# Layer 0 of a two-layer perceiver: where Newton's square root runs, five decode steps for fourteen, and the order of a turn

## The chip, the core and the metric

The kernel runs on one core of one Trainium2 chip, written in Bass with the Tile framework. The metric is the device time of one launch in microseconds (us), median of several runs. The engines are named as in the profile: PE (TensorE, matmuls), DVE (VectorE), ACT (ScalarE), POOL (GpSimd) and SP (SyncE, here only a queue that issues DMAs).

## What is computed

The input x is 64 sequences of 32 places with 256 features, and each sequence has a context of 257 places. Six blocks are added to x one after the other, each on its layer norm. Cut to what matters here:

```
def _layernorm(x, axis=-1, eps=1e-05):
    return (x - m) / jnp.sqrt(v + eps)
...
x = x + _L0_xattn_ref(_layernorm(x, axis=-1), ctx_1024, ctx_1024, ...)
x = x + _L0_attn_ref(_layernorm(x, axis=-1), ...)
x = x + _L0_ffn_ref(_layernorm(x, axis=-1), ...)
x = x + _L1_xattn_ref(_layernorm(x, axis=-1), ctx_1024, ctx_1024, ...)
x = x + _L1_attn_ref(_layernorm(x, axis=-1), ...)
x = x + _L1_ffn_ref(_layernorm(x, axis=-1), ...)
return x
```

The first is a cross-attention with 16 heads of 16 and a causal window, so that only the first 32 places of the context count; the second a causal self-attention of the same shape; the third a linear layer with inputs and weights in fp8 (e4m3). Layer 1 has a cross-attention over all 257 places, a gated mixer and a mixture of one shared and the best 2 of 8 experts. The fp8 weight comes as bytes and is decoded on the chip: sign, four exponent bits and three mantissa bits become a number. In both attentions of layer 0 keys and queries are turned by the rotary tables: `near * cos + far * sin`, where `far` is the partner feature.

## The kernel before

The 2048 rows of x are four tiles `xs[g]` of 512 rows. `small_attentions` (L246) runs both attentions of layer 0 as one pipeline over eight groups: `order` lists (attention 0, g = 0 to 3) and then (attention 1, g = 0 to 3). A group n has four turns, t = 0 to 3; each turn scores 128 rows. All instructions of layer 0 are kept in the order in which the program issues them, on each engine (`InOrder`, `kept`), and `line` carries the last tiles from turn to turn. In a turn the loop (L560 to L626) does this for different tiles at once:

- `turned` (transposes of e, ps_t, copied to eT by ACT) and, at the turn's end, `context` (ps_o, then o on DVE) for the tile of two turns ago; `by_feature` (transposes of o, ps_c, copied to cT by ACT) for the one of three turns ago; `project` (ps_p, added to x by DVE) for the one of four turns ago.
- `rotated` for the group after: keys in t 0 and 1, queries in t 2 and 3. PE makes ps_qk, DVE `part` (times sin), SP copies `part` to `far` with four DMAs, ACT makes `near`, POOL multiplies it by cos. The addition `near + far` into kT or qT, on POOL, is returned as a function and issued one turn later (`adds`, `due`), behind the next turn's own `near` except at t = 0. Before the first group everything of `rotated` but far and the sum is on DVE.
- `spread_keys`: kT times the heads' masks into kb, three of four on ACT, one on POOL.
- `values` for the group after, at t 0 and 2: ps_v, copied to v by ACT, written to `v_rows` by SP; `blocks` reads them back into the block-diagonal vb, four DMAs for each half, both halves at t = 3.
- `norm_steps` for the group after the next: mean and variance on DVE (st, mv), then 1/sqrt by three Newton steps on 128x4 numbers (ve, half, r, sq, rn), then y on DVE. Newton runs on DVE for the first two groups and in group 0, otherwise on POOL. `prepare` takes a step at t 0, 1, 2 and 3 each. `opened` transposes y (psT) into yT at t = 3.
- `scores` (pair_bank; mx and sc on DVE; e on ACT), and `sums` for the last tile (sm on DVE).
- `decode_fp8`: a step at t 0 and 2, in groups 6 and later at every t. It has fourteen steps, seven for each of two halves of 256 columns, in the tile `scratch`; the result is w8.

In group 6 the fp8 layer's own steps for rows 0 (`first_sides`) come in, and from group 7 on `cross_attention` takes over PE, two steps a turn: keys and values of the last context place, the four pieces of the first keys (`keys`), queries. After the pipeline, cross-attention, mixer and experts follow from 237 us on. `first_loads` is a generator of DMAs on SP: three steps before the loop, then one a turn at t 1 to 3.

Of the kernel before, what the change touches and what calls it, by code (L numbers as in the profile page):

```python
# [16 lines left out]
P = 128  # L17
# [47 lines left out]
def perceiver_kernel(ctx: ExitStack, tc: tile.TileContext, a: dict, out: bass.AP):  # L65
# [54 lines left out]
    def turn(ps, src, eye):  # L120
        return kept(nc.tensor.transpose(ps, src, eye))  # L121

    def norm_steps(g, eng=None, apart=False, ts=range(NT), by_act=False):

        x = xs[g]
        n, t0 = len(ts), ts[0]
        st = small.tile([P, n, 6], F32, tag="st", name="st")
        mv = small.tile([P, n, 2], F32, tag="mv", name="mv")
        for t in range(n):
            vector.bn_stats(st[:, t, :], x[:, t0 + t, :])  # L130
        if apart:
            yield
        for t in range(n):
            vector.bn_aggr(mv[:, t, :], st[:, t, :])

        ve = small.tile([P, n], F32, tag="ve", name="ve")
        vector.tensor_scalar(ve, mv[:, :, 1], EPS, None, ALU.add)
        half = small.tile([P, n], I32, tag="half", name="half")
        vector.tensor_scalar(half, ve.bitcast(I32), 1, None, ALU.logical_shift_right)
        r0 = small.tile([P, n], I32, tag="r0", name="r0")  # L140
        vector.tensor_scalar(r0, half, -1.0, float(0x5F3759DF), ALU.mult, ALU.add)
        r = r0.bitcast(F32)
        for _ in range(3):
            sq = small.tile([P, n], F32, tag="sq", name="sq", bufs=6)
            rn = small.tile([P, n], F32, tag="rn", name="rn", bufs=6)
            if eng is vector:
                vector.tensor_tensor(sq, r, r, ALU.mult)
                vector.scalar_tensor_tensor(sq, sq, -0.5, ve, ALU.mult, ALU.mult)
                vector.scalar_tensor_tensor(rn, sq, 1.5, r, ALU.add, ALU.mult)
            else:  # L150
                gpsimd.tensor_tensor(sq, r, r, ALU.mult)
                gpsimd.tensor_tensor(sq, sq, ve, ALU.mult)
                gpsimd.tensor_scalar(sq, sq, -0.5, 1.5, ALU.mult, ALU.add)
                gpsimd.tensor_tensor(rn, sq, r, ALU.mult)
            r = rn
        if by_act:
            off = small.tile([P, n], F32, tag="off", name="off")
            gpsimd.tensor_scalar(off, mv[:, :, 0], -1.0, 1.0, ALU.mult, ALU.mult)
            gpsimd.tensor_tensor(off, off, r, ALU.mult)
        yield  # L160
        y = ypool.tile([P, n, D], F32, tag="y", name="y")
        for t in range(n):
            if by_act:
                scalar.activation(
                    y[:, t, :],
                    x[:, t0 + t, :],
                    AF.Identity,
                    bias=off[:, t : t + 1],
                    scale=r[:, t : t + 1],
                )  # L170
            else:
                vector.tensor_scalar(
                    y[:, t, :],
                    x[:, t0 + t, :],
                    mv[:, t, 0:1],
                    r[:, t : t + 1],
                    ALU.subtract,
                    ALU.mult,
                )
            if t == 1 and n > 2:  # L180
                yield
        return y
# [63 lines left out]
    def small_attentions(layers, first_loads, decode, sides, load_layer1, layer1):  # L246
# [54 lines left out]
            if not it["from_ctx"]:  # L301
                it["kvT"] = yT

        def rotated(it, i, c):

            src, cs, sn = (
                (it["kvT"], cos, sin) if i == 1 else (it["yT"], cosq, sinq)
# [5 lines left out]
            w, v0 = it["w"], it["v0"]  # L313
            ps = pa([P, GT], "ps_qk")
            proj(ps, lambda k: w[:, i, k, c * P : (c + 1) * P], lambda k: src[:, k, :])

            def by_place(table):
                return table.rearrange("p (o q) -> p o q", o=1).to_broadcast([P, 16, S])
# [2 lines left out]
                return tile_.rearrange("p (b q) -> p b q", q=S)  # L321

            bias = vec[:, v0 + 2 * i + c : v0 + 2 * i + c + 1]
            part = part_([P, GT], "part")
            vector.scalar_tensor_tensor(
                by_seq(part), by_seq(ps), bias, by_place(sn), ALU.add, ALU.mult
            )
# [2 lines left out]
            for at in range(0, P, S):  # L330
                queue = scalar if (it["n"], i, c) == (0, 0, 1) and at >= 2 * S else sync
                queue.dma_start(out=far[at : at + S, :], in_=part[at ^ S : (at ^ S) + S, :])
            near = near_([P, GT], "near")
            if it["n"] > 0:
                scalar.activation(near, ps, AF.Identity, bias=bias)
                gpsimd.tensor_tensor(by_seq(near), by_seq(near), by_place(cs), ALU.mult)
# [166 lines left out]
        it = group(0, fetch(0))  # L503
        next(loads)
        after = group(1, fetch(1))
        next(loads)
        for half in range(2):
            clear(vbs[0][half], vector)
            clear(vbs[1][half], gpsimd)
# [5 lines left out]
        opened(it)  # L515
        mask(1)
        vector.tensor_tensor(eye, ident[:, 0:S], ident[:, 64 : 64 + S], ALU.add)
        steps = norm_steps(order[1][1], vector, apart=True)
        next(steps)
        adds.append(rotated(it, 1, 1))  # L520
        adds[0]()
# [1 line left out]
            spread_keys(it, 0, 0, part)  # L523
        adds.append(rotated(it, 0, 0))
        adds.append(rotated(it, 0, 1))
        adds[1]()
        for part in range(2):
            spread_keys(it, 0, 1, part)
# [1 line left out]
            add()  # L530
        for pair in range(2):
            values(it, pair)
        after["y"] = finish(steps)
        for half in range(2):
            blocks(it, half)
        now = it


# [3 lines left out]
        for n in range(len(order) + 1):  # L542
# [3 lines left out]
                after["kb"] = [None, None]  # L546
            kvT = coming = None
            if n + 2 <= last:
                side = norm_steps(order[n + 2][1], None if n else vector, apart=True)
            else:  # L550
                side = sides

            def prepare(at):
                if n + 2 <= last and at:
                    try:
                        next(side)
                    except StopIteration as end:
                        return end.value

            for t in range(NT):  # L560
                if line[2]:
# [2 lines left out]
                if n <= last:  # L564
                    if t < 2:
                        kb_now = (now, 1, t)
                    elif after is not None:
                        kb_now = (after, 0, t - 2)
                due, adds = adds, []
                if t == 0:  # L570
                    for add in due:
                        add()
                    due = []
                if kb_now:
                    spread_keys(*kb_now, 0)
                if line[4]:
# [1 line left out]
                if after is None:  # L578
                    next(layer1, None)
                else:  # L580
                    y = prepare(t % 2 == 1)
                    adds.append(rotated(after, *((1, 0), (1, 1), (0, 0), (0, 1))[t]))
                if line[3]:
                    by_feature(line[3])
                prepare(t % 2 == 0)
                if n + 2 > last:
                    next(side, None)
                    next(side, None)
                if n > 0:
                    add_bias(n - 1, t)  # L590
                if n > 0 and (t % 2 == 0 or n + 2 > last):
                    next(decode, None)
                for add in due:
                    add()
                if kb_now:
                    spread_keys(*kb_now, 1)
                if after is None:
                    next(layer1, None)
                elif t % 2 == 0:
                    values(after, t // 2)  # L600
                    if (n, t) == (0, 0):
                        opened(after)
                elif t == 3:
                    for half in range(2):
                        blocks(after, half)
                    if n + 2 <= last:
                        coming = group(n + 2, kvT)
                        coming["y"] = y
                        opened(coming)
                line[0] = scores(now, t) if n <= last else None  # L610
                if (n, t) == (last, NT - 1):
                    pair_pool.close()
# [19 lines left out]
    def first_loads():  # L632
# [12 lines left out]
        sync.dma_start(out=xs[1], in_=x_view[1])  # L645
        yield
        sync.dma_start(out=xs[2], in_=x_view[2])
        sync.dma_start(out=w_cur[:, 3], in_=a["w_l0x"][:, 3])
        row_load(R_XO0)
        sync.dma_start(out=xs[3], in_=x_view[3])  # L650
        yield
        sync.dma_start(out=raw, in_=a["w_fp8"])
        for at in (R_AO0, R_FF, R_XO1, R_GO):
            yield
            row_load(at)
        for i in range(0, 4, 2):
# [9 lines left out]

    def decode_fp8():

        scratch = sb.tile([P, 4, D], F32, tag="yT", name="scratch")
        u, neg, e_f, scale = (scratch[:, i, :] for i in range(4))  # L670
        bits = scale.bitcast(I32)
        for c in range(2):
            vector.tensor_copy(u, raw[:, c * D : (c + 1) * D])
            vector.tensor_scalar(neg, u, 128.0, None, ALU.is_ge)
            yield
            vector.scalar_tensor_tensor(u, neg, -128.0, u, ALU.mult, ALU.add)
            vector.tensor_copy(bits, u)
            yield
            vector.tensor_scalar(bits, bits, 3, None, ALU.logical_shift_right)
            vector.tensor_copy(e_f, bits)  # L680
            yield
            vector.scalar_tensor_tensor(u, e_f, -8.0, u, ALU.mult, ALU.add)

            vector.tensor_scalar(bits, e_f, 1.0, 120.0, ALU.max, ALU.add)
            yield
            vector.tensor_scalar(bits, bits, 23, None, ALU.logical_shift_left)

            vector.tensor_scalar(e_f, e_f, 1.0, None, ALU.min)
            yield
            vector.scalar_tensor_tensor(u, u, 0.125, e_f, ALU.mult, ALU.add)  # L690
            vector.tensor_tensor(u, u, scale, ALU.mult)
            yield
            vector.tensor_scalar(neg, neg, -2.0, 1.0, ALU.mult, ALU.add)
            vector.tensor_tensor(w8[:, c, :], u, neg, ALU.mult)
            yield

    def linear(g):

# [329 lines left out]
    def cross_attention(loaded):  # L1028
# [283 lines left out]
        last_rows(2, vl)  # L1312
        yield
        yield
        yield
        yield
        fetched.append(fetch_context(1))
        now = fetched.pop(0)
        last_column(now)
        mask_rows(now)  # L1320
        for piece in range(4):
            keys(now, piece)
            yield
        yT = by_feature(first_y[0])
        yield
        qT = qT_([P, 2, GT], "qT")
# [727 lines left out]
```

## Time and profile before

| | us |
|---|---|
| three runs: median, lowest, highest | 929.02, 928.76, 929.92 |
| profiled execution, and its span | 928.56, 926.8 |
| first score matmuls of group 0 | 30.4 |
| group 0 to group 1, first scores to first scores | 20.4 |
| groups 1 to 5, the same | 24.5, 24.8, 24.9, 24.9, 25.0 |
| group 6, the same | 30.0 |
| group 7 to the first scores of layer 1 | 32.4 |

Of the span PE is busy 92%, DVE 65%, ACT 46%, POOL 54%. A busy PE need not be at its peak, and idle time of an engine costs only where the next work of the bounding engine waits for it. So the table cuts layer 0 at the first score matmul of each group, and inside a stretch the timeline of PE shows each idle time with what ended it in brackets. L106 and L118 are the lines of helpers through which all instructions go; the tiles' names tell them apart. In a timeline a line gives start, duration, engine, operation, what is written and read, the shapes and the count.

### The profile page before, as it was taken

Reading aid. Unit: us, or ns where it says so; the run is one execution under the profiler, and the core shown is the slowest. Engines: PE = TensorE matmul, PEld = TensorE weight load, DVE = VectorE, ACT = ScalarE, POOL = GpSimd, SP = SyncE. Lnnn points to the kernel's source line nnn. Section 1 sums busy time; section 2 is a strip of 40 time slices with the busy share of each in tenths; the row PEclk is TensorE's granted clock in tenths of the full one; section 3 lists DMA queues with packets and bytes.
Section 4 is the critical chain, followed back from the end, with each engine's and each line's share of the span. In section 5 each row is a group of like instructions: output and inputs, shape, how many; then the busy total and the mean of one; then the engine's idle time right before and its main releaser. Section 6 shows DMA issues by size and latency. Waiting matters only on the chain. (4 is left out here: it accounts for less than half of the span.)

```text
span 926.8 us, 22828 instructions
## 1 busy us (share of the span) xinstructions
PE 856.0 (92%) x8699; PEld 588.5 (63%) x8699; DVE 605.3 (65%) x1755; ACT 424.1 (46%) x1099; POOL 501.1 (54%) x982
## 2 busy tenths in 40 slices
PE   6899999979899999999999999999889889999993
PEld 3566666656456666666656666565656648888882
DVE  7888888897677677675777666878654872111116
ACT  2566666645555555554555456564443212222210
POOL 3567667764674656564664747656531214555430
PEclk9999999989999999999999999999799979999997
DMA  7445333543110111111110112000001046777758
GB/s 240 140 133 141 85 88 101 132 115 104 53 52 8 46 53 53 52 54 52 53 52 3 52 52 98 2 2 24 2 23 35 24 143 189 235 240 229 216 182 272
DMA packets 66926, 88.79 MB, mean 96 GB/s; under 512 B 32480, under 2 KB 50688, under 8 KB 64768
## 3 DMA queue, kind: packets, MB, share of 16 engines
q1 hardware_dynamic: 63264, 77.75, 27.6%
q0 software_dynamic: 3456, 9.44, 3.1%
q8 instruction: 69, 1.13, 0.5%
q14 instruction: 41, 0.34, 0.1%
q10 hardware_dynamic: 96, 0.13, 0.1%
HBM read 65.80 MB, written 13.11 MB: 85 GB/s over the span
## 5 line engine op out<-in xcount | busy, mean ns | idle before, releaser
L106 ACT ACTIVATE e<-e,xnm 128x257 f32<-128x257 f32 x256 | 127.2, 498 | 51.5 <-DVE xnm L106 45.5
L106 DVE CUSTOM_DVE_ANT_0 e<-ps_s,mask 128x257 f32<-128x257 f32 x256 | 93.5, 421 | 49.6 <-PE ps_s L118 47.9
L118 PE MATMUL ps_k<-ct,w_w_l1x 128*128 128x512 f32 x256 | 122.3, 600 | 1.6 <-ACT yT L106 0.6
L106 POOL TENSOR_SCALAR e<-e,xsm 128x256 f32<-128x256 f32 x256 | 121.8, 496 | 0.0
L118 PE MATMUL ps_v<-w_w_l1x,ct 128*128 128x256 f32 x512 | 121.8, 381 | 0.0
L121 PE MATMUL ps_t<-cst,e 128*128 128x128 f32 x640 | 102.9, 284 | 7.8 <-DVE eT L106 6.9
L106 DVE COPY eT<-ps_t 128x512 f32<-128x512 f32 x128 | 88.0, 687 | 30.3 <-PE ps_t L121 30.1
L118 PEld LDWEIGHTS ps_v<-w_w_l1x,ct 128*128 128x128 f32 x512 | 93.9, 191 | 11.0 <-issue 0.2
L106 POOL TENSOR_TENSOR x<-x,rows 128x256 f32<-128x256 f32 x96 | 71.3, 759 | 46.2 <-ACT y L106 19.4
L106 ACT ACTIVATE kT<-ps_k,vec 128x512 f32<-128x512 f32 x64 | 44.1, 689 | 100.5 <-PE ps_k L118 100.3
L121 PEld LDWEIGHTS ps_t<-cst,e 128*128 128x128 f32 x640 | 72.1, 142 | 26.4 <-DVE eT L106 7.8
L106 ACT ACTIVATE hTr<-ps_h,w 128x256 f32<-128x256 f32 (+1 forms) x80 | 31.4, 450 | 115.0 <-issue 82.7
L106 DVE TENSOR_TENSOR og<-ps_o,b 128x512 f32<-128x512 f32 (+1 forms) x20 | 12.8, 638 | 105.6 <-PE ps_o L118 105.6
L118 PEld LDWEIGHTS ps_k<-ct,w_w_l1x 128*128 128x128 f32 x256 | 44.5, 190 | 41.3 <-issue 35.3
L1817 POOL DMA_INDIRECT r_rows<-og,lv x36 | 35.6, 989 | 60.9 <-DVE og L106 56.0
L118 PE MATMUL ps_h<-ygT,w 128*128 128x256 f32 (+1 forms) x320 | 65.8, 359 | 0.6 <-issue 0.6
L118 PE MATMUL ps_o<-w,hTr 128*128 128x256 f32 x288 | 65.3, 379 | 0.0
L106 ACT COPY v<-ps_v 128x512 f32<-128x512 f32 x80 | 46.4, 582 | 39.5 <-PE ps_v L118 39.4
L106 POOL TENSOR_TENSOR last<-e,xsm 128x4 f32<-128x4 f32 x64 | 13.0, 204 | 88.4 <-DVE xsm L106 88.0
L118 PEld LDWEIGHTS ps_h<-ygT,w 128*128 128x128 f32 x320 | 54.9, 190 | 6.6 <-issue 0.8
L118 PEld LDWEIGHTS ps_o<-w,hTr 128*128 128x128 f32 x288 | 54.4, 190 | 7.2
L106 ACT ACTIVATE kb<-kT,cst 128x256 f32<-128x256 f32 x96 | 45.4, 512 | 26.7 <-POOL kT L106 25.1
(210 smaller groups left out, 1677.2 us busy)
## 6 DMA issues: line engine op xcount, KB each, us to landing
ct<-in_ctxT SPq DMA_DIRECT2D x16, 1024.0 KB, 5.4
w<-in_ew SPq DMA_DIRECT2D x20, 514.0 KB, 3.6
w<-in_ew SPq DMA_DIRECT2D x20, 512.0 KB, 3.7
far<-part SPq DMA_DIRECT2D x126, 64.0 KB, 2.3
v_rows<-v SPq DMA_DIRECT2D x16, 256.0 KB, 2.3
vb<-v_rows SPq DMA_DIRECT2D x64, 64.0 KB, 2.1
r<-r_rows SPq DMA_DIRECT2D x8, 512.0 KB, 8.2
b<-in_eb SPq DMA_DIRECT2D x20, 128.0 KB, 3.8
```

The source lines that it names most:

```text
L106: ins = getattr(self.engine, name)(*args, **kw)
L118: return kept(nc.tensor.matmul(ps, **args))
L121: return kept(nc.tensor.transpose(ps, src, eye))
L1817: wrote = nc.gpsimd.indirect_dma_start(out=r_rows, out_offset=bass.IndirectOffsetOnAxis(ap=write_i[:, at : at + 1], axis=0), in_=o[:, i, : ...
```

## The change

Layer 0 is issued in another order, and two pieces of work are done in another way.

- Newton's steps run on DVE in all groups of layer 0. `norm_steps` can stop once more, ahead of Newton (`split`), and the steps are taken at other places: the statistics at t = 0, mean to r at t = 1 before `rotated`, Newton and the first half of y at t = 2 behind `rotated`, the other half of y at t = 3 (in group 0 at t 1, 2 and 3).
- `decode_fp8` has five steps over all 512 columns, one a group at t = 0: seven DVE instructions instead of 28.
- `by_feature`: in odd turns its transposes follow ps_qk and its two copies on ACT go before `near`; in even turns they follow `values`, and the copies go behind `near`, kb and v.
- All additions of a turn are issued at the start of the next.
- The second half of vb is read at t = 1 of the group itself, group 0's first half at its t = 0; the heads' `opened` of group 1 goes from t = 0 to t = 1 of group 0.
- Before the loop, the keys' `part` and `near` take tiles of their own (`spare`), and x2, w 3, a row of biases and x3 are loaded one step, then one turn, at a time.
- The first piece of layer 1's keys is made at t = 1 of group 7, the second at t = 2 and two at t = 3; before it was one at t = 2, two at t = 3 and one at t = 0 after it.

```diff
@@ norm_steps
+        if split:
+            yield
         for _ in range(3):
@@ rotated(it, i, c, between=None)
             proj(ps, lambda k: w[:, i, k, c * P : (c + 1) * P], lambda k: src[:, k, :])
+            if between:
+                by_feature(between)
+            spare = (it["n"], i) == (0, 1)
...
-            part = part_([P, GT], "part")
+            part = sb.tile([P, GT], F32, tag=f"sc{c}", name="part") if spare else part_([P, GT], "part")
...
-            near = near_([P, GT], "near")
+            near = sb.tile([P, GT], F32, tag=f"e{c}", name="near") if spare else near_([P, GT], "near")
@@ before the loop
         after = group(1, fetch(1))
-        next(loads)
...
-        steps = norm_steps(order[1][1], vector, apart=True)
+        steps = norm_steps(order[1][1], vector, apart=True, split=True)
+        next(steps)
         next(steps)
...
         adds.append(rotated(it, 0, 1))
+        next(steps)
         adds[1]()
...
+        next(loads)
         after["y"] = finish(steps)
-        for half in range(2):
-            blocks(it, half)
@@ the loop over groups and turns
-                side = norm_steps(order[n + 2][1], None if n else vector, apart=True)
+                side = norm_steps(order[n + 2][1], vector, apart=True, split=True)
...
+            ahead, behind = ((0, 1, 0, 1), (1, 0, 2, 0)) if n else ((0, 0, 0, 2), (0, 1, 2, 0))
...
-                due, adds = adds, []
-                if t == 0:
-                    for add in due:
-                        add()
-                    due = []
+                for add in adds:
+                    add()
+                adds = []
...
-                    y = prepare(t % 2 == 1)
-                    adds.append(rotated(after, *((1, 0), (1, 1), (0, 0), (0, 1))[t]))
-                if line[3]:
+                    y = prepare(ahead[t])
+                    turns = None if t % 2 == 0 else line[3]
+                    adds.append(rotated(after, *((1, 0), (1, 1), (0, 0), (0, 1))[t], turns))
+                if line[3] and after is None:
                     by_feature(line[3])
-                prepare(t % 2 == 0)
+                prepare(behind[t])
...
-                if n > 0 and (t % 2 == 0 or n + 2 > last):
+                if n > 0 and t == 0:
                     next(decode, None)
-                for add in due:
-                    add()
...
                     values(after, t // 2)
-                    if (n, t) == (0, 0):
-                        opened(after)
+                    if line[3]:
+                        by_feature(line[3])
+                elif (n, t) == (0, 1):
+                    opened(after)
                 elif t == 3:
-                    for half in range(2):
-                        blocks(after, half)
+                    blocks(after, 0)
...
+                if n <= last and t == 1:
+                    blocks(now, 1)
+                if (n, t) == (0, 0):
+                    blocks(now, 0)
@@ first_loads
         sync.dma_start(out=xs[2], in_=x_view[2])
+        yield
         sync.dma_start(out=w_cur[:, 3], in_=a["w_l0x"][:, 3])
         row_load(R_XO0)
+        yield
         sync.dma_start(out=xs[3], in_=x_view[3])
@@ decode_fp8, the new body
+        vector.tensor_copy(bits, raw)
+        vector.tensor_scalar(
+            bits, bits, 127, 20, ALU.bitwise_and, ALU.logical_shift_left
+        )
+        yield
+        vector.tensor_scalar(bits, bits, float(120 << 23), None, ALU.add)
+        yield
+        vector.tensor_scalar(v, u, -(2.0**-6), 0.0, ALU.add, ALU.min)
+        yield
+        vector.tensor_tensor(u, u, v, ALU.add)
+        yield
+        vector.tensor_scalar(v, raw, 128.0, -2.0, ALU.is_ge, ALU.mult)
+        vector.scalar_tensor_tensor(
+            w8.rearrange("p c d -> p (c d)"), v, 1.0, u, ALU.add, ALU.mult
+        )
+        yield
@@ cross_attention
-        yield
-        yield
-        fetched.append(fetch_context(1))
         now = fetched.pop(0)
         last_column(now)
         mask_rows(now)
-        for piece in range(4):
+        keys(now, 0)
+        yield
+        yield
+        fetched.append(fetch_context(1))
+        for piece in range(1, 4):
             keys(now, piece)
             yield
+        yield
```

More of the change, by code (lines that the diff above doesn't have):

```diff
@@ L121, in turn, with norm_steps @@
         return kept(nc.tensor.transpose(ps, src, eye))
-    def norm_steps(g, eng=None, apart=False, ts=range(NT), by_act=False):
+    def norm_steps(g, eng=None, apart=False, ts=range(NT), by_act=False, split=False):
         x = xs[g]
@@ L302, in opened, with rotated @@
                 it["kvT"] = yT
-        def rotated(it, i, c):
+        def rotated(it, i, c, between=None):
             src, cs, sn = (
@@ L548, in small_attentions, with prepare @@
             if n + 2 <= last:
-                side = norm_steps(order[n + 2][1], None if n else vector, apart=True)
+                side = norm_steps(order[n + 2][1], vector, apart=True, split=True)
             else:
                 side = sides
-            def prepare(at):
-                if n + 2 <= last and at:
+            def prepare(count):
+                y = None
+                for _ in range(count if n + 2 <= last else 0):
                     try:
@@ L557, in prepare @@
                     except StopIteration as end:
-                        return end.value
+                        y = end.value
+                return y
+            ahead, behind = ((0, 1, 0, 1), (1, 0, 2, 0)) if n else ((0, 0, 0, 2), (0, 1, 2, 0))
             for t in range(NT):
@@ L652, in first_loads @@
         sync.dma_start(out=raw, in_=a["w_fp8"])
-        for at in (R_AO0, R_FF, R_XO1, R_GO):
+        row_load(R_AO0)
+        for at in (R_FF, R_XO1, R_GO):
             yield
@@ L667, in decode_fp8 @@
     def decode_fp8():
[L669 to L674, printed above, removed]
-            yield
-            vector.scalar_tensor_tensor(u, neg, -128.0, u, ALU.mult, ALU.add)
-            vector.tensor_copy(bits, u)
-            yield
[L679 to L695, printed above, removed]
+        scratch = sb.tile([P, 2, 2 * D], F32, tag="yT", name="scratch")
+        u, v = (scratch[:, i, :] for i in range(2))
+        bits = u.bitcast(I32)
+        vector.tensor_copy(bits, raw)
[14 more added lines that the diff above has]
+        yield
     def linear(g):
@@ L1314, in cross_attention @@
         yield
+        now = fetched.pop(0)
+        last_column(now)
+        mask_rows(now)
+        keys(now, 0)
         yield
@@ L1317, in cross_attention @@
         fetched.append(fetch_context(1))
-        now = fetched.pop(0)
-        last_column(now)
-        mask_rows(now)
-        for piece in range(4):
+        for piece in range(1, 4):
             keys(now, piece)
             yield
+        yield
         yT = by_feature(first_y[0])
```

## The prediction

> **What bounds the kernel now.** The page's chain of waits reaches back only to 761 us, into the experts, which the change leaves alone. So I read layer 0 in stretches cut at the first score matmul of each group (group n = 0 to 7, turns t0 to t3), and then the engines' timelines where TensorE stood idle. The stretches (columns: length, then busy PE, PEld, DVE, ACT, POOL, granted clock, DMA share, GB/s):
>
> ```profile
> 50.78:75.28 24.50, 23.23 (x370) 16.09 (x370) 20.81 (x48) 15.74 (x37) 17.46 (x29) 1.00 0.48 129
> 100.12:124.97 24.85, 23.50 (x370) 16.01 (x370) 20.88 (x48) 15.77 (x37) 17.60 (x29) 1.00 0.34 87
> ...
> 174.90:204.85 29.95, 22.59 (x366) 15.81 (x366) 29.31 (x58) 15.07 (x36) 24.27 (x38) 0.94 0.42 107
> 204.85:237.25 32.40, 31.92 (x460) 20.61 (x459) 24.34 (x59) 13.83 (x31) 11.68 (x26) 0.95 0.38 122
> ```
>
> Groups 1 to 5 are TensorE's, with 1.3 to 1.5 us missing in each. Group 6 is VectorE's: 29.31 of 29.95 us. After it TensorE is full again. The missing 1.3 us lie in turn t2 (timelines of PE, ACT and DVE, group 3):
>
> ```profile
> 107.97 1.13 PE L118 MATMUL ps_p<-w_w_l0x,cT 128*128 128x256 f32 x4 [1.26 <-ACT cT L106]
> ...
> 106.71 0.69 ACT L106 ACTIVATE near<-ps_qk,vec 128x512 f32<-128x512 f32 x1 [1.74 <-POOL sq L106]
> 107.30 0.62 ACT L106 ACTIVATE cT<-ps_c,vec 128x128 f32<-128x128 f32 x2
> ...
> 105.85 0.75 DVE L106 SCALAR_TENSOR_TENSOR part<-ps_qk,vec,cst 128x512 f32<-128x512 f32 x1
> ```
>
> TensorE waits for cT, cT stands behind near on ACT, and near starts when part ends, here as in every turn (POOL's sq was not what it needed). Part was late by a decode step and the norm's small operations. Group 6 (PE and DVE):
>
> ```profile
> 202.63 0.69 PE L121 MATMUL ps_c<-cst,o 128*128 128x128 f32 x2 [3.50 <-DVE o L106]
> ...
> 182.75 1.54 DVE L106 TENSOR_SCALAR scratch<-scratch 128x256 int32<-128x256 int32 x2
> ...
> 198.71 0.81 DVE L106 TENSOR_SCALAR scratch<-scratch 128x256 f32<-128x256 f32 x1
> 199.55 1.36 DVE L106 TENSOR_TENSOR w<-scratch 128x256 bf16<-128x256 f32 x1
> ```
>
> Four of the fourteen decode steps (scratch, w) stand in the queue that TensorE waits for. Last, the one place where Newton's square root already runs on VectorE while POOL works (DVE, then POOL):
>
> ```profile
> 23.44 0.16 DVE L106 TENSOR_TENSOR sq<-rn 128x4 f32<-128x4 f32 x1
> 23.64 1.19 DVE L106 SCALAR_TENSOR_TENSOR sq<-sq,ve 128x4 f32<-128x4 f32 x1
> 24.86 1.19 DVE L106 SCALAR_TENSOR_TENSOR rn<-sq,rn 128x4 f32<-128x4 f32 x1
> 26.09 0.41 DVE L106 TENSOR_TENSOR sq<-rn 128x4 f32<-128x4 f32 x1
> ...
> 23.54 2.50 POOL L106 TENSOR_TENSOR qT<-near,far 128x512 f32<-128x512 f32 x2 [1.82 <-DVE rn L106]
> 26.01 0.48 POOL L106 TENSOR_SCALAR kb<-kT,cst 128x256 f32<-128x256 f32 x1
> ```
>
> The same 128x4 operation takes 0.16 us, or until POOL's running instruction ends (24.83, 26.05, 26.50 against POOL's 24.8, 26.04, 26.49): one operation for each POOL instruction.
>
> **Start and group 0.** Removed from SP ahead of the first far copies: x2, w 3, a row, x3 (1.3 MB, issued from 5.84 to 8.90; DMA above 330 GB/s until 16). The first far copies, issued by 14.14, landed at 17.90; without the loads they should land 2.1 us after the last issue (page: 2.3 for far), at 15.7. The keys' part and near take spare tiles, so the queries' part no longer waits 2.25 us for a buffer (18.08 becomes 16.1). SP's fourteen far issues at 0.62 us then set the pace: the last lands near 23.9 and its add ends near 25.2 to 25.7 (26.04 before). The heads' transposes (psT) leave the place before the first scores, where they waited 1.41 and 1.52 us, so these start near 25.7 instead of 30.38: -4.7. Part is given back. In t1 yT now follows near and two kb on ACT (0.6 + 0.85 + 1.05 us), about 1.5 us later than t2's ps_qk could start. x2, loaded behind the v copies near 24.9, needs 3.9 us as x0 did. All of group 2's y (1.4 us) falls into t3, behind POOL's add, kb and near: some 2.5 us ahead of psT, of which 1.7 are new. I take -4.7 + 1.5 + 0.8 (half of the 1.7, since y was partly in t3 before) = -2.4; bounds -5.0 (nothing given back; the clock of 0.66 in the stretch 30 to 35, where four ps_qk took 3.44 us and not 1.88, may also go) and 0 (all given back).
>
> **Groups 1 to 5.** (a) In odd turns cT goes ahead of near on ACT: it needs only ps_c, so t2's ps_p starts 0.49 us after ps_t as elsewhere, and not 1.92: -1.5 with the 0.1 us of its slower first matmul. In even turns cT goes behind near, two kb and v: part 0.67 + 0.6 + 0.85 + 0.5 + 0.6 = 3.2 us after ps_qk, where TensorE has ps_v 1.82, ps_c 0.22, scores 0.69, ps_o 0.59, ps_t 0.49 = 3.8 before ps_p. Covered, with 0.6 to spare; a part later than that stalls ps_p by the rest. (b) Decoding: 2.76 us a group before (13.8 over five, by the groups by form), now one step of 512 columns in t0, 0.6 to 1.5 us: hidden. (c) Newton leaves POOL (12 operations, 3.3 us of t1) for VectorE: 9 operations at 0.20 = 1.8 us if free (33.76 to 35.50), in t2 behind part. Behind it on DVE stand y 0 and 1, mx, sc, o, sm, x, y 2 and 3: 0.75 + 0.72 + 0.61 + 0.33 + 0.71 + 0.17 + 0.28 + 0.75 = 4.3 us, and psT in t3 waits for the last y, ps_c for o. From ps_qk's end that is 0.77 + N + 4.3 for DVE; TensorE has 3.8 + ps_p 0.87, ps_qk 1.72, ps_c 0.22, half of psT 0.49 = 7.1. So N up to 2.0 us costs nothing, and every us beyond it costs one. (d) The adds move ahead of near on POOL. Far lands 3.9 to 5.6 us after part, so t1's add starts about 0.8 us into Newton and is followed without a gap by kb, near and the bias: 1.28 + 0.48 + 1.29 + 0.73 = 3.8 us. Bounds of N: 1.8 (POOL idle) and 4.8 (these four let one operation each pass, five are free). I take 4.1, what the row nearest to it took (22.85 to 26.93, three of nine held): stall 2.1, group -1.5 + 2.1 = +0.6, five groups +3.0; bounds -7.5 and +6.5. (e) Half the vb copies (4 x 0.5 us on SP) move from t3 to t1: t0's far is issued sooner, t2's up to 2 us later, whose add waits on POOL in t3 ahead of nothing that t3 needs; the half itself is read three turns on. Nothing.
>
> The Trainium skill has a rule that speaks against (c): "SBUF — State Buffer", section "Who interferes with whom", says that a DVE instruction with two SBUF inputs contends with a GpSimd one that reads SBUF, and that the loser fully blocks for the whole instruction. The rows above agree (1.19 us instead of 0.16). By the rule alone N would be at its upper end in every group, and the sum some 3.5 us higher; by the prologue's row it is what I take.
>
> **Group 6 and the turn to layer 1.** Decoding ends in group 5, so DVE's queue from 173 to 209 loses 0.55 + 1.47 + 1.2 + 2.13 = 5.35 us (176.32, 182.75, 190.54, 198.71). Only the first 0.1 meets a wait for ps_qk. ps_p in t3 comes 1 us later by (a), still ahead of DVE. -5.2; bounds -6.5 (part of the 0.66 clock of 200 to 210 goes too) and -2 (POOL, 24.3 us busy there, holds the other operations longer). Keys of layer 1: four pieces of 1.72 us, the first a turn and a half earlier, among the same TensorE work, which fills 31.92 of 32.40 us: 0, bounds +-0.5. Its context is fetched some 6 us before, by the page 5.4 from issue to landing.
>
> **Sum.** Against the profiled execution (928.56; span 926.8 and 1.76 around it): -2.4 + 3.0 - 5.2 = -4.6, 924.0. The median is 0.46 above the profiled execution: 924.4.
>
> **Rivals.** *Newton runs free*: t1's part is so late that the add comes after Newton. For: far took up to 5.6 us. Against: it would have to be 1 us later than in most rows. -2.4 - 7.5 - 5.2 = -15.1: 913.9. *The port decides, slower*: N at 4.8 and each half of y stuck too (0.95 at 111.53 against 0.41: +0.55 each): stall 3.9, group +2.4, five +12.0; total +4.4: 933.4. For: POOL's four instructions without a gap. Against: y finds POOL waiting for t2's far. It decides once the stall passes 1.5 + 7.6 / 5 = 3.0 us a group. *No net change*: the start gives all back and group 6 yields 2: 0 + 3.0 - 2 = +1.0: 930.0. That cT isn't moved is excluded: in the program's order it stands before near in odd turns.
>
> **Chances.** Forecast 0.44 (own range 919 to 928), free Newton 0.24, slower 0.18, no change 0.14. A measurement of this kernel tells 0.2% (1.9 us) from nothing: faster is the free Newton and most of the forecast, 0.64; same 0.16, with the forecast's upper edge; slower 0.20. The range takes in the free Newton and half of the slower rival: 912.5 to 931.5.
>
> **What would show it.** First scores near 26; no idle of ps_p on cT in t2; sq and rn rows of 0.5 to 1.3 us on DVE in t2, and psT or ps_c in t3 waiting for DVE's y or o about 2 us; groups 1 to 5 near 25.4 us (23.4 if Newton is free, over 26.5 if the port decides); group 6 near 24.7 with no scratch rows. Wrong would be a group 0 that takes as much longer as the scores start earlier, or ps_p waiting for cT in odd turns t1 and t3, because v and kb now stand before it.

## The result, and the profile after

The changed kernel is slower by 1.1%: 939.56 us (median of six, 935.87 to 942.43) against 929.46 of the kernel before in the same comparison (928.76 to 931.1), ratio 1.0106 with a 95% interval of 1.0081 to 1.0132. The profiled execution took 938.01 us, its span 936.2. The stretches of layer 0, cut as before at the first score matmul of each group, here groups 1, 3, 6 and 7 (columns: length, busy PE, PEld, DVE, ACT, POOL, granted clock, DMA share, GB/s):

```profile
48.10:76.57 28.47, 24.38 (x370) 16.16 (x369) 24.12 (x56) 15.76 (x37) 16.93 (x19) 1.00 0.43 113
...
102.85:130.00 27.15, 25.14 (x369) 17.44 (x368) 23.52 (x54) 16.01 (x37) 14.89 (x17) 0.94 0.31 82
...
184.57:210.68 26.11, 22.50 (x365) 15.54 (x364) 23.97 (x49) 14.15 (x34) 21.93 (x36) 0.93 0.39 107
210.68:245.80 35.12, 32.77 (x460) 20.35 (x459) 25.41 (x61) 15.07 (x34) 13.25 (x28) 0.95 0.42 127
```

DVE's busy time in groups 1 to 5 rose from 20.8 us to 23.5 to 24.3, time in which an operation is held included; that is more than the 23 us that TensorE's matmuls of a group take when nothing waits (22.96 in experiment 1). Cut finer, at the first scores of every turn (the second turn is t1 to t2, the third t2 to t3):

| | before | after | difference | forecast |
|---|---|---|---|---|
| start and group 0 | 50.78 | 48.10 | -2.7 | -2.4 |
| groups 1 to 5, t1 to t2 | 39.8 | 32.2 | -7.6 | -7.5 |
| the same, t2 to t3 | 27.7 | 43.8 | +16.1 | +10.5 |
| the same, t3 to the next t0 | 33.3 | 34.9 | +1.6 | 0 |
| the same, t0 to t1 | 23.3 | 25.5 | +2.2 (group 1 alone) | 0 |
| group 6 | 29.95 | 26.11 | -3.8 | -5.2 |
| group 7 to layer 1's first scores | 32.40 | 35.12 | +2.7 | 0 |
| from there to the end | 689.5 | 690.4 | +0.9 | 0 |

The third turn holds the loss. DVE, then POOL, in t2 of group 3 (timelines: start, duration):

```profile
112.06 0.75 DVE L106 SCALAR_TENSOR_TENSOR part<-ps_qk,vec,cst 128x512 f32<-128x512 f32 x1
...
113.50 0.16 DVE L106 SCALAR_TENSOR_TENSOR sq<-sq,ve 128x4 f32<-128x4 f32 x1
113.70 1.26 DVE L106 SCALAR_TENSOR_TENSOR rn<-sq,rn 128x4 f32<-128x4 f32 x1
114.99 0.41 DVE L106 TENSOR_TENSOR sq<-rn 128x4 f32<-128x4 f32 x1
115.44 1.21 DVE L106 SCALAR_TENSOR_TENSOR sq<-sq,ve 128x4 f32<-128x4 f32 x1
116.68 0.65 DVE L106 SCALAR_TENSOR_TENSOR rn<-sq,rn 128x4 f32<-128x4 f32 x1
117.37 0.74 DVE L106 TENSOR_SCALAR y<-x,mv,rn 128x256 f32<-128x256 f32 x2
118.02 0.69 DVE L106 TENSOR_REDUCE mx<-pair_bank 128x16 f32<-128x512 f32 x1
```

```profile
113.66 1.27 POOL L106 TENSOR_TENSOR kT<-near,far 128x512 f32<-128x512 f32 x1 [1.58 <-ACT near L106]
114.92 0.47 POOL L106 TENSOR_SCALAR kb<-kT,cst 128x256 f32<-128x256 f32 x1
115.36 1.26 POOL L106 TENSOR_TENSOR near<-near,cst 128x512 f32<-128x512 f32 x1
116.59 0.72 POOL L106 TENSOR_TENSOR x<-x,rows 128x256 f32<-128x256 f32 x1
```

Five of the nine operations pass in 0.16 us, and four are held, each until one of POOL's four instructions ends (114.96 against 114.93, 115.40 against 115.39, 116.65 against 116.62, 117.33 against 117.31). Newton takes 4.6 us here and 4.5 to 4.6 in the four other groups, with four held in each. What TensorE pays (PE, same turn, then all of groups 1 to 5 as sums of waits):

```profile
119.82 0.44 PE L121 MATMUL ps_c<-cst,o 128*128 128x128 f32 x2 [1.41 <-DVE o L106]
120.09 0.60 PE L121 MATMUL psT<-cst,y 128*128 128x128 f32 x4
121.29 0.87 PE L121 MATMUL psT<-cst,y 128*128 128x128 f32 x4 [0.60 <-DVE y L106]
...
123.29 1.08 PE L118 MATMUL ps_o<-vb,eT 128*32 128x64 f32 x32
```

```profile
PE ps_c L121 <- DVE o L106: 7.4, 6, 1.5
PE psT L121 <- DVE y L106: 3.2, 6, 0.6
PE pair_bank L118 <- POOL qT L106: 1.5, 1, 1.5
```

In each group ps_c waits for o some 1.4 us and psT for the last y 0.6; before, ps_p's wait for cT (1.3 to 1.4 us) was the only long one of groups 1 to 5. In groups 3 and 4 the granted clock was also lower after these waits (0.53 to 0.61, last section): the 32 ps_o matmuls take 1.08 us and not 0.65.

### The profile page after: what moved, and what is told of

Same layout as the page of the kernel before. It is cut to its first block, busy times and chain, and to the rows that moved or that the text cites. A ratio compares the mean times of both kernels' runs of the same rounds, so it can differ in the third digit from the quotient of the medians.

```text
span 936.2 us, 22786 instructions
## 1 busy us (share of the span) xinstructions
PE 863.7 (92%) x8699; PEld 592.2 (63%) x8699; DVE 616.3 (66%) x1779; ACT 424.7 (45%) x1099; POOL 486.1 (52%) x922
## 5 line engine op out<-in xcount | busy, mean ns | idle before, releaser
L106 POOL TENSOR_TENSOR x<-x,rows 128x256 f32<-128x256 f32 x96 | 71.7, 763 | 43.2 <-ACT y L106 19.5
L106 POOL DMA_INDIRECT yg<-y_rows,lv x36 | 35.1, 975 | 39.8 <-DVE lv L106 29.1
```

The lines of the kernel that those rows point to most:

```text
L106: ins = getattr(self.engine, name)(*args, **kw)
```

## Experiments

Ratios are to the kernel before in the same comparison; group lengths come from each run's profile.

**1. Newton back on POOL in the changed kernel.**

```diff
-side = norm_steps(order[n + 2][1], vector, apart=True, split=True)
+side = norm_steps(order[n + 2][1], None if n else vector, apart=True, split=not n)
-ahead, behind = ((0, 1, 0, 1), (1, 0, 2, 0)) if n else ...
+ahead, behind = ((0, 1, 0, 1), (1, 0, 1, 0)) if n else ...
```

> The changed kernel, but Newton's square root of groups 1 to 5 back on POOL in t1, unsplit, as before the change; all else of the change stays. Theory A (VectorE's nine 128x4 operations get stuck behind POOL's instructions in t2 and make o and y late in t3): the third turn falls from 8.2 to 9.3 us to about 5.6, groups 2 to 5 from 26.3 to 27.8 us to about 23.4, group 1 from 28.5 to about 25.5 (the late load of the fp8 weights stays); 17 us in all: 921 us. Theory B (the long third turn comes from the new order of adds, half blocks or cT): it stays above 8 us and the time at 936 to 940.

Measured: 921.73 us, ratio 0.9896 [0.9869, 0.9924]. Groups 3 and 4, and the waits of PE in groups 1 to 5:

```profile
97.83:121.03 23.20, 23.19 (x370) 16.25 (x369) 19.71 (x45) 16.01 (x37) 18.32 (x31) 1.00 0.37 99
121.03:143.99 22.96, 22.96 (x370) 16.29 (x369) 19.84 (x45) 16.00 (x37) 17.36 (x29) 1.00 0.37 94
```

```profile
PE pair_bank L118 <- POOL qT L106: 1.5, 1, 1.5
PE ps_p L118 <- ACT cT L106: 0.2, 1, 0.2
```

Theory A holds: the third turn is 5.53 to 6.02 us in groups 2 to 5, TensorE has no idle time left in group 4, and the rest of the change is worth 8 us.

**2. Newton on VectorE alone, in the kernel before** (the split, and one more step taken in t2 behind part).

```diff
-side = norm_steps(order[n + 2][1], None if n else vector, apart=True)
+side = norm_steps(order[n + 2][1], vector, apart=True, split=n > 0)
...
+if n > 0 and t == 2:
+    prepare(True)
 prepare(t % 2 == 0)
```

> The kernel before with one part of the change alone: Newton of groups 1 to 5 on VectorE behind part in t2. Theory A: the rows of sq and rn take up to 1.3 us each, ending with POOL's instructions, o and y are late in t3, groups 1 to 5 go from 24.9 to 26.5 to 28 us: 937 to 944 us. Theory B (the move alone is harmless, and only together with the new order does it cost): POOL has 3.3 us less in t1 and the groups stay at 24.9 or fall a little: 926 to 930 us.

Measured: 948.42 us, ratio 1.02 [1.0176, 1.0225], above the range of theory A. Each of groups 1 to 5 takes 28.2 to 29.2 us; PE's waits in them:

```profile
PE ps_c L121 <- DVE o L106: 9.2, 5, 2.0
PE ps_p L118 <- ACT cT L106: 6.4, 5, 1.4
PE psT L121 <- DVE y L106: 3.5, 5, 0.7
```

The old wait for cT stays and the new ones come on top. Newton takes 4.4 us, three operations held, with POOL's adds in their old place: the new order is not what holds it. The move costs 18.7 us here and 17.8 in the changed kernel (939.56 against the 921.73 of experiment 1).

**3. cT ahead of near in odd turns alone, and with it the decoding in five steps** (both on the kernel before, Newton on POOL; e8 adds the change's `decode_fp8` and its place).

```diff
+turns = None if t % 2 == 0 else line[3]
-adds.append(rotated(after, ...))
-if line[3]:
+adds.append(rotated(after, ..., turns))
+if line[3] and (after is None or t % 2 == 0):
     by_feature(line[3])
...
-if n > 0 and (t % 2 == 0 or n + 2 > last):
+if n > 0 and t == 0:               # e8
     next(decode, None)
```

> The kernel before with one part alone: in odd turns cT stands ahead of near on ACT. If the wait of ps_p for cT in t2 is all that is missing there: 1.5 us off each of groups 1 to 5 and part of group 6, 920 to 922 us. If the stall only moves (near, kb or v late, so that t3's or t0's first matmuls wait): 927 to 930 us.

> The kernel before with two parts: cT ahead of near in odd turns, and the fp8 decoding in five steps, one in t0. With cT alone the 1.5 us won in the second turn came back as 1.25 us in the third (5.53 to 6.80). Theory A (it came back because the two decoding operations in t2, 1.4 us, then make y and o late): the third turn falls to 5.5 to 5.7, groups 1 to 5 to 23.0 to 23.2 and group 6 by 5: 916 to 920 us. Theory B (it came back because POOL's adds behind near or its near itself are late): the third turn stays at 6.8, only group 6 gains: 922 to 924 us.

Measured: 927.76 us, 0.9968 [0.9955, 0.9981]; with the decoding 922.10, 0.9917 [0.9896, 0.9937]. The first came out as its second theory says: the second turn falls from 7.92 to 6.39, but the third grows from 5.53 to 6.7 to 6.8, where ps_p waits 0.99 us for the cT of the even turn. That cT keeps its old place behind near; what is late is near, and not for want of part, which ends at 110.74. Ahead of near on ACT stands a kb that waits for kT, whose addition on POOL comes behind Newton, near and the bias of t1 and ends at 113.07 (ACT, group 3 of e4):

```profile
113.11 0.51 ACT L106 ACTIVATE kb<-kT,cst 128x256 f32<-128x256 f32 x1 [3.27 <-POOL kT L106]
113.52 0.67 ACT L106 ACTIVATE near<-ps_qk,vec 128x512 f32<-128x512 f32 x1
```

In the kernel before this kb was waited for in the same way (ACT idle for 2.66 us), but TensorE came 1.5 us later. With the new decoding ps_p's wait is 0.35 us in group 3, and the third turn 6.14 to 7.11: the time is theory B's, the turn lies between the two. Groups 1 to 5 together are 3.1 and 4.0 us shorter than before. In the changed kernel with Newton on POOL the third turn is down to 5.53 in groups 3 and 4. There that addition stands ahead of Newton, and ACT does not wait ahead of the kb of t2 (107.03 in group 3). So the rows point at the new order of the additions for the rest; it was not tried alone. The second run also shows what a shorter group 6 is worth: it falls to 24.3 us, but the stretch behind it grows from 32.4 to 35.8.

**4. Newton on VectorE at three other places in the changed kernel**: ahead of t2's part; behind t1's part (with a fourth version that has experiment 6's other edits too); in t2 behind mx, sc, o and sm.

```diff
-(0, 1, 0, 1), (1, 0, 2, 0)
+(0, 1, 1, 1), (1, 0, 1, 0)     e6: ahead of part, t2
+(0, 1, 0, 1), (1, 1, 1, 0)     e9, e10: behind part, t1
...
         sums(line[1])
+    if n > 0 and t == 2:        # e15, and not behind rotated
+        prepare(behind[t])
```

> The changed kernel with Newton still on VectorE, but one step sooner in its queue: ahead of t2's part and not behind it, where POOL stands idle before its next add. Theory A (the cost is the collision with POOL's four instructions): the nine operations take 0.16 to 0.2 us each, 1.8 us in all, the third turn falls to 6 us or less, but part is 1.8 us late and cT behind it has 0.6 us to spare, so the second turn's end pays up to 1.2 us: groups 2 to 5 at 23.5 to 25 us, 925 to 932 us. Theory B (the cost is nine more instructions in VectorE's queue, wherever they stand): the groups stay at 26 to 28 us, 936 to 942 us.

> The changed kernel with Newton on VectorE one place sooner: behind t1's part, ahead of y's first half one turn later. Theory A (what counts is how much stands between part and o in the same turn while POOL works): POOL has two instructions there (near and x, 1.27 and 0.72 us, after an idle 1.9 us), so N is 3.0 to 3.5 us; o then needs 0.77 + 3.3 + 0.72 + 0.61 + 0.33 = 5.7 us from ps_qk's end, and TensorE asks for it after 6.2 (in t2, with 0.77 + 4.5 + 0.75 + 1.66 = 7.7, it waited 1.44): no stall in t1, t2 like the kernel with Newton on POOL; groups 2 to 5 at 23.0 to 23.7 us, 920 to 924 us. Theory B (nine operations on VectorE cost some 3 us a group wherever they are, as they did ahead of t2's part): groups 2 to 5 at 25.5 to 28, 934 to 941 us.

> The same place for Newton, with layer 1's keys as before, x3 loaded one turn sooner and the first decoding step in t3 of group 1. If theory A of the run ahead holds, as fast as the version with Newton on POOL, 917 to 920 us, with POOL some 3 us a group less busy; by theory B 930 us or more.

> The changed kernel with Newton and the first half of y still on VectorE in t2, but behind mx, sc, o and sm, which read PSUM or were not held in any trace. Theory A (it is the place that costs): these pass while POOL's four instructions run (3.8 us), Newton then starts some 3.3 us after part, when they are nearly done, and takes 1.8 to 2.4 us; ps_c no longer waits for o, the last y comes 1 to 1.5 us sooner, t3's part some 1.3 us late: the third turn falls to 5.8 to 7.0 us, groups 2 to 5 to 23.4 to 24.8, 922 to 930 us. Theory B (nine more operations anywhere in VectorE's queue cost the same): groups 2 to 5 stay at 26 to 28, 935 to 942 us.

Measured: 941.91 us, ratio 1.011 [1.0063, 1.0158]; 943.33, 1.0128 [1.0098, 1.0157]; 936.50, 1.0082 [1.0051, 1.0112]; 940.42, 1.0095 [1.0066, 1.0125]. As a forecast of the time theory A fell in all four; theory B's ranges hold the time of e6, e10 and e15, and e9 lies 2 us above its range. Newton itself did get shorter: 2.8 to 3.1 us ahead of part (1.8 expected; one or two operations were still held), 3.2 to 3.3 as expected for t1, and 1.7 to 3.4 behind the scores. But TensorE waits for something else each time (sums over groups 1 to 5 of e6, of e9 and of e15, a fence each):

```profile
PE ps_p L118 <- ACT cT L106: 13.3, 5, 3.1
```

```profile
PE ps_p L118 <- ACT cT L106: 9.7, 5, 1.9
PE ps_c L121 <- DVE o L106: 4.5, 5, 1.3
```

```profile
PE psT L121 <- DVE y L106: 8.4, 8, 2.1
PE pair_bank L118 <- POOL qT L106: 1.4, 1, 1.4
PE ps_p L118 <- ACT cT L106: 0.6, 2, 0.4
PE ps_c L121 <- DVE o L106: 0.3, 1, 0.3
```

Ahead of part it makes part late, with it near and the cT behind near; a turn sooner it makes o late in t1 and part late in t2; behind the scores o is in time and the last y is not. So held time is not all of the cost: in group 2 of e15 Newton passed unheld in 1.67 us (y's first half moved back with it), and the group still took 24.99 us, where it takes 23.46 with Newton on POOL. At none of the places tried did VectorE's chain through t1 to t3 have a hole for all of Newton.

**5. Fewer iterations** in groups 1 to 5 of the changed kernel. This separates the held operations from any further operation.

```diff
-        for _ in range(3):
+        for _ in range(times):     # 2 in e13, 1 in e14, for n > 0
```

> The changed kernel with two of the three Newton iterations in groups 1 to 5 (the third is left out there, six operations in place of nine). In the changed kernel five operations pass before POOL's add starts and four are held. Theory A (held operations are the cost): the sixth is held until the add ends, y's first half behind it by kb and near, and mx starts 1.3 us sooner than before, which is what ps_c waited for o (1.44 us): the third turn falls from 8.2 to 9.3 us to 5.6 to 6.5, groups 2 to 5 to 23.4 to 24.2, 922 to 927 us. Theory B (each operation costs its share): two thirds of the stall stay, groups 2 to 5 at 25.3 to 26, 932 to 935 us.

> The changed kernel with one of the three Newton iterations in groups 1 to 5 (two left out, three operations in place of nine). Theory A: the three operations pass before POOL's add, N is 0.5 us, y's second quarter is held once: no stall in t3, groups 2 to 5 at 23.0 to 23.6 us, 919 to 923 us, as with Newton on POOL. Theory B: a third of the stall stays, groups 2 to 5 at 24.2 to 24.6, 926 to 929 us.

Measured: 934.80 us, ratio 1.0052 [1.0031, 1.0072]; 924.05, 0.9936 [0.9912, 0.996]. Groups 2 to 5 took 27.0 us on average with nine operations, 25.6 with six, 23.6 with three, 23.3 with Newton on POOL. DVE in t2 (six operations, group 3; then three, group 2):

```profile
113.98 0.16 DVE L106 TENSOR_TENSOR sq<-rn 128x4 f32<-128x4 f32 x1
114.17 1.18 DVE L106 SCALAR_TENSOR_TENSOR sq<-sq,ve 128x4 f32<-128x4 f32 x1
115.39 0.41 DVE L106 SCALAR_TENSOR_TENSOR rn<-sq,rn 128x4 f32<-128x4 f32 x1
115.83 2.07 DVE L106 TENSOR_SCALAR y<-x,mv,rn 128x256 f32<-128x256 f32 x2
```

```profile
84.09 0.16 DVE L106 SCALAR_TENSOR_TENSOR rn<-sq,r 128x4 f32<-128x4 f32 x1
84.29 1.91 DVE L106 TENSOR_SCALAR y<-x,mv,rn 128x256 f32<-128x256 f32 x2
86.12 0.67 DVE L106 TENSOR_REDUCE mx<-pair_bank 128x16 f32<-128x512 f32 x1
```

With six, theory B's number is met, but not its reason: y takes the place of the operations left out and is held instead (2.07 us for two, free 0.74). With three y is held too (1.91), but mx comes soon enough, and the groups are theory A's (23.0 to 23.6, but for group 3 with 24.7; 924.05 us lies a little above its range). From part's end to mx pass 5.2, 4.4 and 2.3 us with nine, six and three operations. Three cost 0.25 us a group, the next three 2.0, the last three 1.4: not a share each, but almost nothing up to a point, and from there roughly the time by which mx comes later (2.1 us, then 0.8; of the 1.4 some 0.5 are the clock in the fourth turns of groups 3 and 4, 7.91 and 7.46 us where six operations leave 6.58).

**6. Layer 1's keys as before, and group 1's loads.** e2 is the changed kernel with the old keys; e5 is experiment 1 with them; e7 adds both edits below to e5, e12 only the second; e11 is e7 with cT ahead of near in every turn of group 6.

```diff
-sync.dma_start(out=w_cur[:, 3], in_=a["w_l0x"][:, 3])
-row_load(R_XO0)
+sync.dma_start(out=xs[3], in_=x_view[3])
 yield
-sync.dma_start(out=xs[3], in_=x_view[3])
+sync.dma_start(out=w_cur[:, 3], in_=a["w_l0x"][:, 3])
+row_load(R_XO0)
 yield
...
-if n > 0 and t == 0:
+if (n > 1 and t == 0) or (n, t) == (1, 3):
     next(decode, None)
```

> The changed kernel with layer 1's keys as they were before the change (four pieces, one a yield, two yields later, the context fetched just ahead). Theory A (spreading the keys puts one piece behind a wait in group 7 and leaves the transposes of layer 1's first y without cover): the stretch from group 7's first scores to layer 1's first scores falls from 35.1 us to about 32.5; 935 to 936 us. Theory B (that stretch is long because of what the groups before it leave behind, the lower clock and x): it stays near 35 and the time at 938 to 940.

> The changed kernel with two parts undone together: Newton of groups 1 to 5 on POOL and layer 1's keys as before. If the two costs are independent, 16 to 18 us and 3 to 4 us come off the changed kernel's 939.6: 917 to 919 us, with the stretch from group 7 to layer 1 at 32.5 to 33 us. If what the keys cost was only the time that DVE lost to Newton in the groups ahead, nothing comes on top: 921 to 922 us.

> Newton on POOL, layer 1's keys as before, and two more edits: x3 is loaded one turn sooner, ahead of w 3 and a row, and the first decoding step stands in t3 of group 1 instead of t0. Theory A (group 1's first turn is long because VectorE waits there for the raw fp8 weights and for x3): that turn falls from 6.35 us to 4.7 to 5.0 and the whole to 1.5 us under the same kernel without the two edits, 916 to 917 us. Theory B (the turn is long because the first far copies land late behind those loads): it stays above 6 us, no gain.

> Newton on POOL, layer 1's keys as before, and of the two edits for group 1 only the one: the first decoding step in t3 of group 1, the loads as the change has them. Theory A (group 1's first turn is long because VectorE waits for the raw fp8 weights): the turn falls from 6.9 to about 4.7 us, and group 0 keeps its 23.5 us, since w 3 is not late: 917 to 918.5 us. Theory B (it is long because far copies and x3 land late, which the load of x3 one turn sooner had mended): it stays at 6.5 to 7 us, 920 to 921 us.

> Newton on POOL, the keys as before, x3 sooner and the decoding step moved, and in group 6 cT ahead of near in every turn. ps_p's wait for cT there (1.95 us) goes. If that wait was what bounds group 6: 27.65 falls to 25.7 us, 916.5 to 917.5 us. If VectorE bounds it (26 of 27 us busy): the wait for o in t3 grows from 1.9 to 3.4 us and more, the group stays at 27.2 or above, 918 to 919 us.

Measured:

| | us | ratio | group 1, t0 to t1 | group 6 | to layer 1 |
|---|---|---|---|---|---|
| e2 | 935.42 | 1.0071 [1.005, 1.0092] | 7.07 | 26.8 | 33.1 |
| e5 | 920.91 | 0.9903 [0.9882, 0.9923] | 6.93 | 27.3 | 33.0 |
| e7 | 918.63 | 0.9876 [0.9858, 0.9894] | 4.66 | 27.7 | 33.1 |
| e12 | 918.59 | 0.9893 [0.9875, 0.9912] | 6.14 | 26.0 | 33.8 |
| e11 | 919.49 | 0.9889 [0.9866, 0.9912] | 4.66 | 27.1 | 32.9 |

The old keys shorten the stretch to layer 1 by 2.05 us (e2 against the changed kernel) and 1.04 (e5 against e1), but the medians fell by 4.1 and 0.8, with intervals that overlap: the stretches put the size at 1 to 2 us, the medians leave it open, and the two parts do not simply add up. The reason is seen in PE's timeline of the changed kernel, and of e2 below it:

```profile
234.47 0.87 PE L121 MATMUL psT<-cst,y 128*128 128x128 f32 x4 [1.04 <-DVE y L106]
235.53 0.33 PE L121 MATMUL psT<-cst,y 128*128 128x128 f32 x1 [0.19 <-DVE y L106]
236.27 0.55 PE L121 MATMUL psT<-cst,y 128*128 128x128 f32 x3 [0.41 <-DVE y L106]
```

```profile
235.91 0.55 PE L121 MATMUL psT<-cst,y 128*128 128x128 f32 x3 [0.34 <-DVE y L106]
```

The piece of keys that stood here moved ahead, and 1.64 us of waiting for layer 1's first y took its place, where e2 waits 0.34: from the last turn's first scores to layer 1's pass 15.47 us with the piece and 15.48 without. Group 1's first turn is mended by both edits (4.66) and hardly by the later decoding step alone (6.14, from 6.93): the sooner load of x3 makes the difference of 1.5 us between e12 and e7. In the changed kernel and in e12 pair_bank waits there for qT (1.51 and 1.25 us), whose addition on POOL waits for far; in e7 it does not. So most of it is the late far copies, with a share for the raw weights. But e7 gave 1.7 us back in group 0, where the clock fell in the last turn, so e7 and e12 cannot be told apart in time. In group 6 ps_p's wait for cT, 1.9 us in e7, is gone in e11, and ps_c's longest for o grew from 1.9 to 3.9 us: VectorE bounds that group. e7 and e12 are the fastest versions measured, 1.1 to 1.2% under the kernel before.

## Why the prediction was wrong

**Right.** Start and group 0 in sum (the scores start 5.5 us sooner for the 4.7 forecast, and group 0 gives back 2.8 for 2.3: the two errors cancel in part); the place of cT in odd turns (-7.6, forecast -7.5); that Newton would be held by POOL in t2, that ps_c and psT would pay in t3, and that the rows would show it.

**The step that failed** is (c) with (d): N at 4.1 us "what the row nearest to it took", stall 2.1, group +0.6. The prologue's row had three of nine operations held. The prediction itself found that the adds moved ahead of near put four POOL instructions in a row without a gap, and four were held in every group: N was 4.5 to 4.6, the stall by its own formula 2.5. The third turn grew by 2.7 to 3.75, 3.2 on average. Of the remainder the trace shows ps_p's wait of 0.58 us in group 5 and slower matmuls behind the waits (four psT in 0.87 to 1.22 us, 0.60 for the four ahead of them). Five groups: +16.1 for +10.5. Then two terms that the sum lacked: the clock in t3 of groups 3 and 4 (+1.6), and group 1's loads (+2.2), which the start section had moved a turn or two later without asking what waits for them. The profiled execution is 14.0 us above the 924.0 forecast for it: 5.6 in the third turns, 3.8 in the clock and the loads, 1.4 in group 6, 2.7 in the stretch behind it and 0.9 after that, less 0.4 elsewhere.

One reading behind (a) was also wrong. That near starts when part ends "here as in every turn" is not so in t2 of the kernel before: in group 3 part ended near 111.6, and near started at 112.78, behind the kb that waits for kT (experiment 3). The changed kernel, with its new order of additions, does not show this wait (near starts at 112.90, part ends at 112.81); the prediction did not count it among what (a) needs.

**The rival "the port decides, slower"** put the groups at +12.0 in all; they came to +12.35. That they agree is luck: it has +19.5 in the third turns, which grew by 16.1, and neither the clock nor the loads. Its mechanism was right that four operations of N are held (4.5 us, not its 4.8) and wrong in y, which in the changed kernel is mostly free behind POOL's last instruction (0.74 us for two) and is held only when Newton is short (experiment 5). It missed the total by 6 us, mostly in group 6 and the stretch behind it.

**Group 6** fell by 3.8 and not 5.2, and the keys were put at 0 with bounds of 0.5 on the ground that TensorE was full there. It was full because of that piece of keys, which covered y: the cover was named in no step. Group 6 and the stretch behind it together won 1.1 us in the changed kernel and 2.0 to 2.2 with the old keys (e5 and e8): what VectorE leaves out of group 6 comes back as waits in group 7.

**The decoding** was costed at nothing in t0, rightly, but what it takes off VectorE was not counted as part of what makes (a) work: with the old decoding the third turn of groups 2 to 4 took back 1.15 to 1.26 us of cT's 1.5, with the new one 0.6 to 0.9 (experiment 3), though 1.5 to 1.6 in groups 1 and 5.

The rule of the Trainium skill weighed in the prediction ("SBUF — State Buffer", "Who interferes with whom") put the sum 3.5 us higher, near 928; the row of the prologue was followed instead, and the runs lie beyond both. The same section says that an operation with one SBUF input escapes only outside the two-port modes, which it says `tensor_scalar` can enter. The trace agrees: y on 128x256 is held (2.07 us for two, free 0.74), while mx, sc and o, which read PSUM, keep their 0.69, 0.69 and 0.41 us beside POOL.

## What to carry to other kernels

Before work is moved to an engine that is 85% busy, follow that engine's own chain through the whole period: if none of its products has time to spare, another place in its queue only moves the wait (here the versions with Newton on VectorE at four places lie between 936.5 and 943.3 us). Count a small SBUF-to-SBUF operation on VectorE by the POOL instructions that run beside it, one for each, and not by its duration alone. When matmuls are moved ahead, look for what was waiting behind them.

## What was not expected of the hardware

That nine 128x4 operations, 1.7 us when they are free, cost 3.6 us a group (17.8 us over five). And that after a wait of 1.4 and one of 0.6 us the granted clock falls in some groups and not in others. Group 3 of the changed kernel behind these waits (stretches; the clock stands after POOL's column):

```profile
122.00:124.00 2.00, 2.00 (x70) 1.51 (x72) 0.73 (x2) 1.69 (x4) 0.92 (x1) 0.53 0.13 33
124.00:126.00 2.00, 2.00 (x23) 1.75 (x16) 1.93 (x5) 1.81 (x5) 1.05 (x2) 0.61 0.40 100
```

Group 2 at 96 to 100 us was granted 1.00 throughout. The drop lasted some 4 us and cost 0.9 to 1.7 us each time (7.91 and 7.46 us for 6.4 to 6.6 in the fourth turn; 8.06 for 6.38 in group 0 of e7, behind a wait of 1.45). In group 3 the waits are 2.0 us, and the third and fourth turn together are 3.8 us longer than before. What picks the groups no run shows.
